# Pairwise products of a batch row: two batch rows at a time, tensor_tensor on VectorE, and less on ScalarE

## The chip, the cores and the metric

The kernel runs on one core of one Trainium2 chip. The metric is device time in microseconds (us) of one execution. A profile, taken in one further execution, records each instruction and each DMA packet. The engines that matter here are VectorE (DVE in the profile), ScalarE (ACT), SyncE (SP, whose queue issues all transfers) and the core's 16 DMA engines.

## The reference

The input is a matrix of 4096 rows (the batch) by 256 columns in float32. For each batch row, every product of two of its elements i and j with j not below i is wanted, in the order of the upper triangle: first the row's element 0 times elements 0 to 255, then element 1 times elements 1 to 255, and so on to element 255 times itself.

```
dot = jnp.einsum('bi,bj->bij', inputs, inputs)     # inputs: (4096, 256) float32
iu, ju = jnp.triu_indices(256)
return dot[:, iu, ju]                              # (4096, 32896) float32
```

The output has 32,896 elements (131,584 bytes) for each batch row, 539 MB in all; the input has 4.2 MB.

## The kernel before

The whole input is held in SBUF, in the tile x. Batch rows lie on the 128 partitions, four neighbouring rows to a partition, so that 512 batch rows make a group and there are eight groups. Three loads on SP's queue (L88) bring the input: group 0, then groups 1 to 3, then groups 4 to 7.

The four output rows of a partition lie one behind the other in HBM, so a group's output is, for each partition, one run of 4 x 32,896 elements. `even_borders` cuts this run into nine pieces of 14,592 or 14,656 elements, regardless of where a row ends. Each piece is made in one buffer of the pool o (three buffers, L79) and written by one transfer from SP's queue (L104): 128 packets of 58,368 or 58,624 bytes, 7,296 or 7,328 KB. Group by group and piece by piece there are 72 pieces. The very first is written in four parts (`FIRST`, L57), so that the first transfer starts early.

`runs` lists the product rows that lie in a piece: product row i of a batch row is x[i] times x[i], x[i+1], up to x[255], so it has 256 - i elements. Each is made by one instruction, in which the factor x[i] is a scalar for each partition. `Shares.multiply` (L44) gives it to VectorE, as a tensor_scalar (L49), or to ScalarE, as an activation with a scale (L52), whichever by its estimate would be done first:

```
v = self.vector + 130 + 0.51 * length
s = self.scalar + 187 + 0.83 * length
```

Both estimates start from zero at each piece (L96). No order is written by hand: each engine takes its instructions in program order, and the tile framework adds the waits. An o buffer can be written again when the transfer that read it has landed; a transfer is issued when both engines have made their part of the piece. SP's queue holds the three loads and then the output transfers in order.

Of the kernel before, what the change touches and what calls it, by code (L numbers as in the profile page):

```python
# [1 line left out]

# [4 lines left out]

F32 = mybir.dt.float32
AF = mybir.ActivationFunctionType
ALU = mybir.AluOpType  # L10

P = 128
UNIT = 64


def even_borders(lo: int, hi: int, pieces: int) -> list[int]:
    units = (hi - lo) // UNIT
    return [lo + units * c // pieces * UNIT for c in range(pieces)] + [hi]


def runs(d: int, lo: int, hi: int):


    width = d * (d + 1) // 2
    for row in range(lo // width, (hi + width - 1) // width):
        at = row * width
        for i in range(d):
            a, b = max(at, lo), min(at + d - i, hi)
            if a < b:
                yield row, i, i + a - at, a, b - a  # L30
            at += d - i


class Shares:


    def __init__(self, nc):
        self.nc = nc
        self.vector = self.scalar = 0.0

    def even(self):
        self.vector = self.scalar = 0.0

    def multiply(self, dst, src, factor, length: int):  # L44
        v = self.vector + 130 + 0.51 * length
        s = self.scalar + 187 + 0.83 * length
        if v <= s:
            self.vector = v
            self.nc.vector.tensor_scalar(dst, src, factor, None, ALU.mult)  # L49
        else:  # L50
            self.scalar = s
            self.nc.scalar.activation(dst, src, AF.Copy, scale=factor)  # L52


REPEAT = 4
PIECES = 9
FIRST = [1024, 3072, 7168]  # L57


@with_exitstack  # L60
def kernel(
    ctx: ExitStack, tc: tile.TileContext, x: bass.AP, out: bass.AP
):

    nc = tc.nc
    n, d = x.shape
    width = out.shape[1]  # L70
    assert n % (P * REPEAT) == 0 and width == d * (d + 1) // 2
    groups = n // (P * REPEAT)
    total = REPEAT * width
    assert total % UNIT == 0
    borders = even_borders(0, total, PIECES)
    slot = max(b - a for a, b in zip(borders, borders[1:]))

    xpool = ctx.enter_context(tc.tile_pool(name="x", bufs=1))
    opool = ctx.enter_context(tc.tile_pool(name="o", bufs=3))  # L79

    x_in = x.rearrange("(g p r) d -> p g r d", p=P, r=REPEAT)
    x_out = out.rearrange("(g p r) c -> g p (r c)", p=P, r=REPEAT)

    xt = xpool.tile([P, groups, REPEAT, d], F32, name="x")
    cuts = sorted({0, 1, groups // 8, groups // 2, groups})
    for a, b in zip(cuts, cuts[1:]):
        if a < b:
            nc.sync.dma_start(xt[:, a:b], x_in[:, a:b])  # L88

    shares = Shares(nc)  # L90
    for g in range(groups):
        for c, (lo, hi) in enumerate(zip(borders, borders[1:])):
            o = opool.tile([P, slot], F32, tag="o", name=f"o_{g}_{c}")
            cuts = [lo, *FIRST, hi] if g == c == 0 else [lo, hi]
            for a, b in zip(cuts, cuts[1:]):
                shares.even()  # L96
                for row, i, j, at, length in runs(d, a, b):
                    shares.multiply(
                        o[:, at - lo : at - lo + length],
                        xt[:, g, row, j : j + length],  # L100
                        xt[:, g, row, i : i + 1],
                        length,
                    )
                nc.sync.dma_start(x_out[g][:, a:b], o[:, a - lo : b - lo])  # L104


# [1 line left out]
_INS = ["r_inputs"]  # L108
_OUTS = [((4096, 32896), "float32")]


# [20 lines left out]
```

## Time and profile before

| | |
|---|---|
| median of 9 runs | 1287.81 us (1287.65 to 1287.94) |
| the profiled execution's own time | 1287.74 us |
| span of its profile | 1286.0 us |
| VectorE busy, instructions | 977.1 us, 4961 |
| ScalarE busy, instructions | 968.3 us, 3299 |
| data moved by DMA, mean rate | 543.71 MB, 423 GB/s |
| issue to landing of a 7,296 KB transfer (median of 39) | 41.9 us |
| issue to landing of a 7,328 KB transfer (median of 32) | 35.9 us |
| first input (512 KB), issue to landing | 3.4 us |

The span runs from the first to the last instruction of the profiled execution; its own time also has what lies before and after. An engine's busy time counts overlapping instructions once, so it can be less than their number times the mean duration of one. "L49 DVE ... o<-x 128x256 f32" reads: line 49 of the kernel, on VectorE, writes tile o from tile x, 128 partitions by 256 elements; "+53 forms" says that the group has other sizes too; behind the bar stand the busy time, the mean duration in ns, and the idle time just before these instructions with what ended it. Of the DMA queues, q1 carries the kernel's own transfers and q14 the engines' instructions. In the table of windows the columns are the stretch, its length, busy time and number of instructions for VectorE, ScalarE and GpSimd, the granted clock of TensorE (not used here), the busy share of the DMA engines and the rate in GB/s.

### The profile page before, as it was taken

To read this page: it belongs to the slowest core of one execution; us is meant where nothing else is said; L and a number is where in the kernel's file an instruction comes from. 1 tells how busy PE (TensorE), PEld (TensorE's weight loads), DVE (VectorE), ACT (ScalarE), POOL (GpSimd) and SP (SyncE) were. 2 spreads that over 40 slices of the span, in tenths; PEclk is the share of its full clock that TensorE was granted. 3 is DMA by queue.
4 is the path that set the end of the run, shared out by engine and by line. 5 is a ranking of instruction groups with operands and counts; after the bars stand their busy time and mean duration, and the time that the engine had idled before them with its cause. 6 is when DMAs were issued, how large, how long until landed. Compare 5 with 4: busy or idle time off the path is not lost.

```text
span 1286.0 us, 8601 instructions
## 1 busy us (share of the span) xinstructions
DVE 977.1 (76%) x4961; ACT 968.3 (75%) x3299; POOL 0.2 (0%) x4
## 2 busy tenths in 40 slices
DVE  8987778777777777777777777777777777688760
ACT  9987778777777777777777777777777777687760
POOL 0000000000000000000000000000000000000000
DMA  9999999999999999999999999999999999999995
GB/s 392 435 435 433 437 431 427 428 431 435 433 435 436 437 435 433 437 426 434 421 435 437 413 433 434 417 430 413 435 410 437 434 411 412 437 435 434 413 408 222
DMA packets 11938, 543.71 MB, mean 423 GB/s; under 512 B 1248, under 2 KB 1248, under 8 KB 2400
## 3 DMA queue, kind: packets, MB, share of 16 engines
q1 hardware_dynamic: 11872, 543.17, 98.0%
q14 instruction: 66, 0.54, 0.1%
HBM read 4.19 MB, written 538.97 MB: 422 GB/s over the span
## 4 chain that ended last, share of the span: by engine, by line
DMA 66%; DVE 31%; issue 0%; DVEq 0%; SPq 0%
DMA out_dram<-o 65%; DVE o L49 31%; DMA x<-in_r_inputs_dram 0%; DVEq L49 0%; SPq L104 0%; DVEq L128 0%
## 5 line engine op out<-in xcount | busy, mean ns | idle before, releaser
L49 DVE TENSOR_SCALAR o<-x 128x256 f32<-128x256 f32 (+53 forms) x4961 | 977.1, 281 | 274.2 <-DMA out_dram<-o 269.9
L52 ACT ACTIVATE o<-x 128x255 f32<-128x255 f32 (+62 forms) x3298 | 967.0, 387 | 282.2 <-DMA out_dram<-o 279.9
L52 ACT ACT_TABLE_LOAD x1 | 1.3, 1283 | 0.7 <-PEq L119 0.7
L119 POOL MEMSET const-bfloat16-1.0<- 128x1 bf16 x1 | 0.1, 102 | 0.0
L119 POOL MEMSET const-uint8-127<- 128x1 uint8 x1 | 0.1, 102 | 0.0
L119 POOL MEMSET const-float32-0.0<- 128x1 f32 x1 | 0.1, 99 | 0.2 <-issue 0.2
L119 POOL MEMSET const-float32-1.0<- 128x1 f32 x1 | 0.1, 99 | 0.0
## 6 DMA issues: line engine op xcount, KB each, us to landing
out_dram<-o SPq DMA_DIRECT2D x39, 7296.0 KB, 41.9
out_dram<-o SPq DMA_DIRECT2D x32, 7328.0 KB, 35.9
out_dram<-o SPq DMA_DIRECT2D x1, 3712.0 KB, 17.8
x<-in_r_inputs_dram SPq DMA_DIRECT2D x1, 2048.0 KB, 12.7
out_dram<-o SPq DMA_DIRECT2D x1, 2048.0 KB, 14.2
x<-in_r_inputs_dram SPq DMA_DIRECT2D x1, 1536.0 KB, 7.2
out_dram<-o SPq DMA_DIRECT2D x1, 1024.0 KB, 12.1
x<-in_r_inputs_dram SPq DMA_DIRECT2D x1, 512.0 KB, 3.4
```

The costliest lines, as they stand in the source:

```text
L49: self.nc.vector.tensor_scalar(dst, src, factor, None, ALU.mult)
L52: self.nc.scalar.activation(dst, src, AF.Copy, scale=factor)
L119: nc = _bacc.Bacc("TRN2", target_bir_lowering=False, num_devices=1)
```

## The change

The layout, the size of the pieces and the way the products are made all change.

- A partition now holds 32 neighbouring batch rows, and a group is two of them (`REPEAT = 2`), so there are 16 groups of 256 batch rows. The input loads are the first group (512 elements for each partition), the rest of the first half, and the second half. The tile x gets one element more, set to zero by a memset.
- A piece is now a stretch of the 32,896 output elements, the same for both batch rows of the group. There are five pieces of 6,528 or 6,592 elements for each batch row; a transfer writes two packets of 26,112 or 26,368 bytes for each partition, and there are 80 pieces. There are still three buffers of o. The first piece is again written in four parts.
- For each block of product rows, `split` gives the first (longest) rows to ScalarE, as few as leave VectorE within `BUDGET` x the number of elements in the block, 1.08 ns for each; in the first piece the two engines are balanced instead.
- `vector_ops` chooses how VectorE makes a product row: "each" is one tensor_scalar for each batch row as before; "all" is one tensor_tensor for both batch rows, whose second operand is x[i] read again and again with a step of zero; "two" is one tensor_tensor that makes product rows i and i+1 of both batch rows. In the last case the pattern has 2 x 2 x (256 - i) elements, although product row i+1 is one shorter: the one element too many is overwritten by the next product row.
- `interleave` cuts the block's rows in two halves and takes VectorE's instructions from them in turn.

The number of bytes moved in and out stays the same, as does the arithmetic of every product.

```diff
--- before.py
+++ after.py
@@ -11,6 +11,10 @@
 
 P = 128
 UNIT = 64
+REPEAT = 2
+PIECES = 5
+BUDGET = 1.08
+FIRST = [512, 1536, 3584]
 
 
 def even_borders(lo: int, hi: int, pieces: int) -> list[int]:
@@ -18,43 +22,75 @@
     return [lo + units * c // pieces * UNIT for c in range(pieces)] + [hi]
 
 
-def runs(d: int, lo: int, hi: int):
+def runs(d: int, lo: int, hi: int) -> list:
 
 
-    width = d * (d + 1) // 2
-    for row in range(lo // width, (hi + width - 1) // width):
-        at = row * width
-        for i in range(d):
-            a, b = max(at, lo), min(at + d - i, hi)
-            if a < b:
-                yield row, i, i + a - at, a, b - a
-            at += d - i
+    found, at = [], 0
+    for i in range(d):
+        a, b = max(at, lo), min(at + d - i, hi)
+        if a < b:
+            found.append((i, i + a - at, a, b - a))
+        at += d - i
+    return found
 
 
-class Shares:
+def vector_ops(block: list) -> list:
 
 
-    def __init__(self, nc):
-        self.nc = nc
-        self.vector = self.scalar = 0.0
-
-    def even(self):
-        self.vector = self.scalar = 0.0
-
-    def multiply(self, dst, src, factor, length: int):
-        v = self.vector + 130 + 0.51 * length
-        s = self.scalar + 187 + 0.83 * length
-        if v <= s:
-            self.vector = v
-            self.nc.vector.tensor_scalar(dst, src, factor, None, ALU.mult)
-        else:
-            self.scalar = s
-            self.nc.scalar.activation(dst, src, AF.Copy, scale=factor)
 
 
-REPEAT = 4
-PIECES = 9
-FIRST = [1024, 3072, 7168]
+
+    ops, k = [], 0
+    while k < len(block):
+        i, j, at, n = block[k]
+        two = k + 2 < len(block) and i == j
+        each = REPEAT * (130 + 0.52 * n)
+        together = 68 + 1.046 * REPEAT * n - (34 if two else 0)
+        if each <= together:
+            ops.append(("each", block[k]))
+        elif two:
+            ops.append(("two", block[k]))
+            k += 1
+        else:
+            ops.append(("all", block[k]))
+        k += 1
+    return ops
+
+
+def interleave(block: list) -> list:
+
+
+    half = len(block)
+    while half and len(vector_ops(block[:half])) > len(vector_ops(block[half:])):
+        half -= 1
+    a, b = vector_ops(block[:half]), vector_ops(block[half:])
+    return [op for k in range(max(len(a), len(b))) for ops in (a, b) for op in ops[k : k + 1]]
+
+
+def vector_time(block: list) -> float:
+    t = 0.0
+    for way, (i, j, at, n) in vector_ops(block):
+        if way == "each":
+            t += REPEAT * (130 + 0.52 * n)
+        else:
+            t += 68 + 1.046 * REPEAT * n * (2 if way == "two" else 1)
+    return t
+
+
+def split(block: list, budget: float) -> int:
+
+
+    scalar, k = 0.0, 0
+    while k < len(block):
+        scalar += REPEAT * (184 + 0.837 * block[k][3])
+        if vector_time(block[k:]) <= budget or scalar > vector_time(block[k + 1 :]):
+            break
+        k += 1
+    return k
+
+
+def window(ap: bass.AP, free: list) -> bass.AP:
+    return bass.AP(ap.tensor, ap.offset, [list(ap.ap[0]), *free])
 
 
 @with_exitstack
@@ -68,40 +104,64 @@
     nc = tc.nc
     n, d = x.shape
     width = out.shape[1]
-    assert n % (P * REPEAT) == 0 and width == d * (d + 1) // 2
+    assert n % (P * REPEAT) == 0 and width == d * (d + 1) // 2 and width % UNIT == 0
     groups = n // (P * REPEAT)
-    total = REPEAT * width
-    assert total % UNIT == 0
-    borders = even_borders(0, total, PIECES)
+    borders = even_borders(0, width, PIECES)
     slot = max(b - a for a, b in zip(borders, borders[1:]))
 
     xpool = ctx.enter_context(tc.tile_pool(name="x", bufs=1))
     opool = ctx.enter_context(tc.tile_pool(name="o", bufs=3))
 
-    x_in = x.rearrange("(g p r) d -> p g r d", p=P, r=REPEAT)
-    x_out = out.rearrange("(g p r) c -> g p (r c)", p=P, r=REPEAT)
+    x_in = x.rearrange("(p r) d -> p (r d)", p=P)
+    x_out = out.rearrange("(p g r) c -> g p r c", p=P, r=REPEAT)
 
-    xt = xpool.tile([P, groups, REPEAT, d], F32, name="x")
-    cuts = sorted({0, 1, groups // 8, groups // 2, groups})
+
+    total = n // P * d
+    xt = xpool.tile([P, total + 1], F32, name="x")
+    nc.vector.memset(xt[:, total:], 0.0)
+    cuts = [0, REPEAT * d, total // 2, total]
     for a, b in zip(cuts, cuts[1:]):
-        if a < b:
-            nc.sync.dma_start(xt[:, a:b], x_in[:, a:b])
+        nc.sync.dma_start(xt[:, a:b], x_in[:, a:b])
 
-    shares = Shares(nc)
     for g in range(groups):
         for c, (lo, hi) in enumerate(zip(borders, borders[1:])):
-            o = opool.tile([P, slot], F32, tag="o", name=f"o_{g}_{c}")
-            cuts = [lo, *FIRST, hi] if g == c == 0 else [lo, hi]
+            o = opool.tile([P, REPEAT, slot], F32, tag="o", name=f"o_{g}_{c}")
+            first = g == c == 0
+            cuts = [lo, *(FIRST if first else []), hi]
             for a, b in zip(cuts, cuts[1:]):
-                shares.even()
-                for row, i, j, at, length in runs(d, a, b):
-                    shares.multiply(
-                        o[:, at - lo : at - lo + length],
-                        xt[:, g, row, j : j + length],
-                        xt[:, g, row, i : i + 1],
-                        length,
+                block = runs(d, a, b)
+                k = split(block, 0.0 if first else BUDGET * REPEAT * (b - a))
+                for i, j, at, length in block[:k]:
+                    for r in range(REPEAT):
+                        row = (g * REPEAT + r) * d
+                        nc.scalar.activation(
+                            o[:, r, at - lo : at - lo + length],
+                            xt[:, row + j : row + j + length],
+                            AF.Copy,
+                            scale=xt[:, row + i : row + i + 1],
+                        )
+                row = g * REPEAT * d
+                for way, (i, j, at, length) in interleave(block[k:]):
+                    at -= lo
+                    if way == "each":
+                        for r in range(REPEAT):
+                            row_r = row + r * d
+                            nc.vector.tensor_scalar(
+                                o[:, r, at : at + length],
+                                xt[:, row_r + j : row_r + j + length],
+                                xt[:, row_r + i : row_r + i + 1],
+                                None,
+                                ALU.mult,
+                            )
+                        continue
+                    m = 2 if way == "two" else 1
+                    nc.vector.tensor_tensor(
+                        o[:, :, at : at + m * length],
+                        window(xt[:, row + j :], [[d, REPEAT], [1, m], [1, length]]),
+                        window(xt[:, row + i :], [[d, REPEAT], [1, m], [0, length]]),
+                        ALU.mult,
                     )
-                nc.sync.dma_start(x_out[g][:, a:b], o[:, a - lo : b - lo])
+                nc.sync.dma_start(x_out[g][:, :, a:b], o[:, :, a - lo : b - lo])
 
 
 # ---- launch: one core; inputs and outputs as the reference has them ----
```

## The prediction

> **What bounds the kernel now.** I read the share of each engine first, then the DMA queues, then the waits, then the trace in windows. From the page of the kernel before:
>
> ```profile
> DVE 977.1 (76%) x4961; ACT 968.3 (75%) x3299; POOL 0.2 (0%) x4
> ...
> q1 hardware_dynamic: 11872, 543.17, 98.0%
> q14 instruction: 66, 0.54, 0.1%
> ...
> L49 DVE TENSOR_SCALAR o<-x 128x256 f32<-128x256 f32 (+53 forms) x4961 | 977.1, 281 | 274.2 <-DMA out_dram<-o 269.9
> L52 ACT ACTIVATE o<-x 128x255 f32<-128x255 f32 (+62 forms) x3298 | 967.0, 387 | 282.2 <-DMA out_dram<-o 279.9
> ```
>
> VectorE and ScalarE idle a quarter of the time, nearly all of it waiting for an output transfer to release one of three o buffers. The 16 DMA engines are 98% busy. So transfers set the time. But a mean hides which engine is last. The windows by stretch (DMA share and GB/s in the last two columns):
>
> ```profile
> 100.00:700.00 600.00, 460.75 (x2338) 456.12 (x1554) 0.00 (x0) 1.00 1.00 433
> 750.00:1250.00 500.00, 382.99 (x1953) 379.19 (x1300) 0.00 (x0) 1.00 0.99 426
> 1271.00:1276.00 5.00, 0.00 (x0) 0.00 (x0) 0.00 (x0) 1.00 0.14 59
> 1277.00:1281.00 4.00, 0.00 (x0) 0.00 (x0) 0.00 (x0) 1.00 0.07 29
> ```
>
> Until 700 us all engines are busy; later the rate drops; after 1271 us two engines work, after 1277 us one (29 GB/s is one sixteenth of the rate). I therefore took from the trace every DMA packet (queue, start, duration, bytes) and the 16 completions of each transfer. How many us the three slowest engines complete after the median one:
>
> | transfer at | slowest (A) | second | third |
> |---|---|---|---|
> | 136 us | 3.6 | 2.0 | 1.2 |
> | 412 us | 10.4 | 6.4 | 4.2 |
> | 688 us | 16.4 | 11.3 | 7.1 |
> | 1252 us | 17.2 | 8.1 | 1.1 |
>
> A loses 2.4 us per 100 us until the others, out of released buffers, must wait for it. The end at 1286 us is A's end. What delays engines is in the packets. A 58,368-byte packet takes 2154 ns. The instruction queue's 8,192-byte packets take 309 ns each, and the data packet right after one takes 440 to 475 ns too long where they follow each other every 33 us (38 times: 4961 VectorE instructions in blocks of 128), and 175 to 200 ns too long where they come every 50 us (24 times: ScalarE). So A carries VectorE's instruction stream at 309+447-4 = 752 ns a block: 22 blocks by 720 us are 16.5 us, against a lag of 17.1. Engine B carries ScalarE's, at 490 ns. A third, C, has no such packets; its data packets are 20 to 60 ns too long, more with more VectorE instructions: mean 29 ns with 8 ending inside a packet, 45 with over 11, and none once both engines have stopped.
>
> [...] queue 14's packets sit between data packets. [...] 433 GB/s is measured from 100 to 700 us[...]. [...] the new distance between partitions is 32 rows of 131,584 bytes, 4 MiB + 16 KiB (before: 512 KiB + 2 KiB).
>
> **The change, part by part.** A's budget before, in us: first packet 3.1; 64 input packets of 159 ns, 9.9; output 1241.1 (8 packets in each of 71 transfers at 2150 or 2160 ns start to start, plus 17.3 for the divided first tile); 78 completions of 5 ns, 0.4; 38 instruction blocks, 28.6. Sum 1283.1; 2.9 us stay unexplained to the span of 1286.0, and I carry them over. The profiled execution took 1287.74, 1.7 outside the span; the median of the runs is 1287.81.
>
> *Smaller packets.* Two rows of 26,112 or 26,368 bytes a partition take the place of one run. From 16,384 bytes in 611 ns and 29,696 in 1100 the slope is 36.73 ns per 1,000 bytes: 968.3 and 977.7 ns, 4 less start to start. Sixteen pairs of rows times 16 packets: 256 x (964.3 + 4 x 973.7) = 1243.9, and 0.1 for the divided first tile: +2.9. Completions and the 6,740 KB transfers hardly count: 86 by 5 ns, 0.4.
>
> *Fewer instructions.* Working the rules of the new planner through: a pair of rows needs 184 VectorE instructions (84 tensor_scalar, 100 tensor_tensor) and 48 on ScalarE; in all 2929 and 786 against 4961 and 3298. 2929/128 is 22.9 blocks; before, 38.8 gave 38, so 22 times 752 ns, 16.5: -12.0. ScalarE's 6 blocks cost B 3 us. C's surplus before is 1276.9-3.1-9.9-1241.1-0.4-2.9 = 19.5 us; by instruction count (3715 of 8259) it becomes 8.8. A stays last: C ends 7.7 us before it. The 752 ns I leave unchanged; if the 447 belonged to the packet's size it would be 200 ns (16.5 falls to 11), and without it A has 7 us and C (8.8) ends last.
>
> *VectorE's work.* Per pair of rows its planned time is 70.3 us (13.8 to 14.2 per tile). tensor_scalar's 130 + 0.52n fits the trace: 4961 x 130 ns plus 0.51 for some 640,000 elements gives 971, measured 977. tensor_tensor is not in the trace. [...] A needs (1244.4+16.5)/16 = 78.8 us per pair. I take the plan, because the trace's tensor_scalars overlap: 281 ns each but 197 busy. All of it then lies beneath the transfers: a tile's product starts when the transfer three back lands and needs 14.2 us, while two transfers of 15.6 stand queued. Without the cover each us over 78.8 counts 16 times. A tensor_tensor of two rows writes one element too many, which the next one overwrites, so each may wait on its forerunner in its half; behind it stands only VectorE's own queue, then SP's output issue. The halves alternate, so another instruction of mostly over 200 ns lies between; [...] I take nothing.
>
> *ScalarE's work* falls to 13.7 us in each pair's 79[...]. *Input:* 2 KB, 14 KB and 16 KB packets, 9.7 against 9.9; first products start about 0.6 us sooner, hidden by input transfers to 12.8 us. *Start:* the first tile's pieces keep their 512 KB, 1, 2 and the rest; VectorE ends it at about 3.6+9.6 = 13.2, the second tile at 27.5[...], while the first tile's transfers end at 28.4: some 0.5 us lost (0 to 2). The memset of one column precedes the first landing.
>
> Sum for A: 3.1+9.7+1244.0+0.4+16.5+2.9+0.5 = 1277.1-1277.3, plus 1.7: **1279.0 us**, 0.7% faster. Its own range is 1271 (C last, no penalty packets) to 1283.
>
> **The rivals.**
> *VectorE becomes the bound.* At 85 ns over the plan per tensor_tensor the pair takes VectorE 78.8 us. A VectorE-bound end has the first input (3.6), the last transfer with its landing (17.5) and 1.7 around it: at that point 1284, then 1.6 us for each further ns. From 89 ns (over 1290.4) it is slower[...]. For it: 100 unseen instructions per pair, each perhaps waiting. Against it: the alternation and the overlap seen. I say 1300 where it happens, chance 0.09.
> *C's surplus doesn't follow the instruction count.* If it is per time VectorE is busy (76% to 88%), 19.5 becomes 22.6: 3.1+9.7+1244+0.4+22.6+2.9+0.5+1.7 = 1285. If per packet, the half-size packets (26 ns each in the trace) say 1280 x 26 = 33 us: 1295.6. Against it: surplus rises with endings at a full VectorE (29 to 45 ns), and is gone in the tail. Chance 0.07.
> *The instruction stream doesn't shrink as counted.* Were each tensor_tensor to bring a wait instruction (1600 more, 35 blocks), A gains 9.8: 1288.8. Before, only some 260 of 8601 are beyond the named groups. Chance 0.04.
> *Row distance.* [...] at a tenth less rate, about 1405. [...] Chance 0.04.
>
> **How the numbers follow.** The forecast has 0.76. Under 0.2% is about what this kernel's measurement can't tell from no change (1285.2 to 1290.4). Faster: 0.75 of the forecast, 0.04 of C's rival: 0.79. Same: 0.01 + 0.01 + 0.03 of the stream's + 0.03 of VectorE's: 0.08. Slower, the rest: 0.13. The range 1271 to 1288 takes in the forecast's own (0.75), C by time, the first of VectorE's and part of the stream's rival: 0.82.
>
> **What would show it.** Queue 14 with some 30 packets, VectorE 2929 instructions and busy near 1120 us, ScalarE 786 and near 226; output packets of 968 and 978 ns; A's lag growing 1.3 us per 100 us and a tail of one engine at about 27 GB/s, some 8 us long. Wrong would be: VectorE without idle on output transfers and DMA share below 0.95 midway (first rival); C last (second); queue 14 above 45 packets (third); DMA full at under 420 GB/s midway (fourth).

## The result, and the profile after

The changed kernel takes 1277.98 us (median of 9 runs, 1277.74 to 1278.24) against 1287.74 us before (29 runs): a ratio of 0.9924, 95% interval 0.9916 to 0.9932. It is 0.76% faster. The prediction was 1279.0 us. The profiled execution took 1277.78 us with a span of 1276.0 us.

From the page of the changed kernel (busy time by engine, the DMA queues, and the groups of instructions):

```profile
DVE 1129.0 (88%) x2978; ACT 234.7 (18%) x787; POOL 0.2 (0%) x4
...
q1 hardware_dynamic: 23008, 543.17, 99.6%
q14 instruction: 32, 0.26, 0.0%
...
L158 DVE TENSOR_TENSOR o<-x 128x104 f32<-128x104 f32 (+60 forms) x1651 | 804.7, 560 | 59.2 <-DMA out_dram<-o 59.2
L137 ACT ACTIVATE o<-x 128x197 f32<-128x197 f32 (+25 forms) x786 | 233.5, 384 | 1000.5 <-DMA out_dram<-o 904.2
L149 DVE TENSOR_SCALAR o<-x 128x216 f32<-128x216 f32 (+5 forms) x1326 | 345.3, 335 | 53.0 <-DMA out_dram<-o 50.0
```

VectorE now works 88% of the time, longer than before, and still waits 109 us for released buffers: the transfers set the time, as before. What fell is the traffic of queue 14, from 66 packets to 32.

The windows of the changed kernel (the last two columns are the DMA share and GB/s):

```profile
100.00:700.00 600.00, 544.76 (x1434) 110.06 (x374) 0.00 (x0) 1.00 1.00 430
750.00:1250.00 500.00, 442.92 (x1182) 93.27 (x318) 0.00 (x0) 1.00 1.00 430
1265.00:1270.00 5.00, 0.00 (x0) 0.00 (x0) 0.00 (x0) 1.00 0.47 200
1271.00:1275.00 4.00, 0.00 (x0) 0.00 (x0) 0.00 (x0) 1.00 0.05 20
```

Two things stand against the windows of before. The rate no longer drops halfway (430 and 430, where it was 433 and 426), because the slowest engine no longer falls so far behind that the others wait for it (7.3 us behind the median engine at the last transfer, where it was 15.0). And the end is still one engine alone, but for some 5 us, where it was some 9. The rate of 430 in the first stretch is lower than the 433 of before; that is the one thing in these lines which the prediction did not have.

The packets of the trace, at the three slowest engines' completions, say the same: A is 1.9 us behind the median engine at 170 us, 4.5 us at 719 us, 7.3 us at the last transfer; the second and third end 2.5 and 1.1 us behind. The trace doesn't name the DMA engine of a packet, but on one engine each packet starts where the one before ends (3 to 4 ns before its recorded end). Followed back in this way from its end, the last engine has the instruction packet of 1233.1 us on it, and behind that a data packet 386 ns too long: VectorE's stream.

### The profile page after: what moved, and what is told of

It is laid out like the page before. It is cut to its first block, busy times and chain, and to the rows that moved or that the text cites. A ratio compares the mean times of both kernels' runs of the same rounds, so it can differ in the third digit from the quotient of the medians.

```text
span 1276.0 us, 4106 instructions
## 1 busy us (share of the span) xinstructions
DVE 1129.0 (88%) x2978; ACT 234.7 (18%) x787; POOL 0.2 (0%) x4
## 4 chain that ended last, share of the span: by engine, by line
DMA 60%; DVE 37%; issue 0%; DVEq 0%; SPq 0%
DMA out_dram<-o 59%; DVE o L158 26%; DVE o L149 11%; DMA x<-in_r_inputs_dram 0%; SPq L164 0%; DVEq L158 0%; DVEq L149 0%; DVEq L188 0%
## 5 line engine op out<-in xcount | busy, mean ns | idle before, releaser
L158 DVE TENSOR_TENSOR o<-x 128x104 f32<-128x104 f32 (+60 forms) x1651 | 804.7, 560 | 59.2 <-DMA out_dram<-o 59.2
L137 ACT ACTIVATE o<-x 128x197 f32<-128x197 f32 (+25 forms) x786 | 233.5, 384 | 1000.5 <-DMA out_dram<-o 904.2
L149 DVE TENSOR_SCALAR o<-x 128x216 f32<-128x216 f32 (+5 forms) x1326 | 345.3, 335 | 53.0 <-DMA out_dram<-o 50.0
```

What stands on the lines that cost most here:

```text
L137: nc.scalar.activation(o[:, r, at - lo : at - lo + length], xt[:, row + j : row + j + length], AF.Copy, scale=xt[:, row + i : row + i + 1],)
L149: nc.vector.tensor_scalar(o[:, r, at : at + length], xt[:, row_r + j : row_r + j + length], xt[:, row_r + i : row_r + i + 1], None, ALU.mult,)
L158: nc.vector.tensor_tensor(o[:, :, at : at + m * length], window(xt[:, row + j :], [[d, REPEAT], [1, m], [1, length]]), window(xt[:, row + ...
```

## The experiments

The theory: the time is that of the DMA engine A which, beside its sixteenth of the data, brings VectorE's instructions. Each block of 128 instructions (38 blocks for 4961 in the kernel before) costs it a packet of 309 ns and a delay of the next data packet (that packet takes longer than others of its size, by 447 ns on average in the kernel before). The change gained by its smaller number of VectorE instructions. The rivals: the layout brought the gain (fewer rows per partition, two packets, another distance of the rows in HBM); the work of VectorE and ScalarE or the number of all instructions matters, not the stream of one engine.

All times are medians of the comparison with the kernel before on the same chip.

| run | us | ratio to before (95% interval) |
|---|---|---|
| changed kernel | 1277.98 | 0.9924 (0.9916 to 0.9932) |
| e1, new layout, old number of instructions | 1290.32 | 1.0020 (1.0012 to 1.0028) |
| e2, other row distance | 1278.82 | 0.9930 (0.9917 to 0.9942) |
| e3, more on VectorE, placed ahead | 1408.89 | 1.0940 (1.0925 to 1.0955) |
| e4, more on ScalarE, placed ahead | 1320.53 | 1.0254 (1.0240 to 1.0268) |
| e5, halves not alternating | 1321.06 | 1.0259 (1.0244 to 1.0274) |
| e6, transfers alone, old layout | 1260.70 | 0.9790 (0.9776 to 0.9805) |
| e7, transfers alone, new layout | 1269.96 | 0.9862 (0.9847 to 0.9877) |
| e8, budget 0.75 | 1274.85 | 0.9900 (0.9883 to 0.9916) |
| e9, no tensor_scalar, budget 0.9 | 1273.26 | 0.9888 (0.9874 to 0.9901) |
| e10, e8 with 1520 more on VectorE | 1282.64 | 0.9961 (0.9948 to 0.9973) |
| e11, e8 with 1520 more on ScalarE | 1278.03 | 0.9925 (0.9911 to 0.9938) |
| e12, old layout, fewer instructions | 1275.96 | 0.9908 (0.9892 to 0.9925) |

### The two halves of the change apart: e1 and e12

e1 keeps the new layout and makes each product by its own instruction, shared evenly between the engines:

```diff
-                block = runs(d, a, b)
-                k = split(block, 0.0 if first else BUDGET * REPEAT * (b - a))
-                ...
+                v = s = 0.0
+                for r in range(REPEAT):
+                    row = (g * REPEAT + r) * d
+                    for i, j, at, length in runs(d, a, b):
+                        ...
+                        if v + 130 + 0.51 * length <= s + 187 + 0.83 * length:
+                            v += 130 + 0.51 * length
+                            nc.vector.tensor_scalar(dst, src, factor, None, ALU.mult)
+                        else:
+                            s += 187 + 0.83 * length
+                            nc.scalar.activation(dst, src, AF.Copy, scale=factor)
```

> The new layout (two rows, five pieces, packets of 26 KB) with one instruction for each product row and batch row, both engines balanced as in the kernel before; so about 4990 VectorE and 3300 ScalarE instructions. Theory (the DMA engine that carries VectorE's instruction stream ends last): 39 blocks in place of 24, at 309 ns and some 366 ns of delay each, 671 ns: 26.2 us in place of 16.1, so 1288 us, and a tail of one engine. Rival (the layout, its packets or the row distance brought the gain): about 1278 us.

It took 1290.32 us. From its page, and its windows at the end:

```profile
DVE 984.5 (76%) x5013; ACT 969.1 (75%) x3315; POOL 0.2 (0%) x4
...
q14 instruction: 68, 0.56, 0.1%
```

```profile
1280.00:1285.00 5.00, 0.00 (x0) 0.00 (x0) 0.00 (x0) 1.00 0.06 26
```

The instruction packets are back (68), and so is an engine that works alone (26 GB/s) until 1287 us. Its last 105 packets contain two instruction packets, and data packets that are 376 to 443 ns too long. The 39 delays of VectorE's stream average 402 ns here, not 366: 39 x (309 + 402 - 4) = 27.6 us, so A's sum is 3.1 + 9.7 + 1244.0 + 0.4 + 27.6 + 2.9 + 1.8 = 1289.5 us. The layout by itself makes the kernel 2.6 us slower (1290.32 against 1287.75); the rival falls.

e12 is the other half: the layout and the packets of before, with tensor_tensors of two product rows of one batch row on VectorE, in alternating halves, and the longest rows of a piece on ScalarE:

```diff
-                shares.even()
-                for row, i, j, at, length in runs(d, a, b):
-                    shares.multiply(...)
+                block = list(runs(d, a, b))
+                scalar = share(block, SCALAR * (b - a) / slot)     # SCALAR = 13500.0, longest rows first
+                ...
+                for m, (row, i, j, at, length) in interleave(rest):
+                    ...
+                        nc.vector.tensor_tensor(
+                            dst,
+                            window(xf[:, base + j :], [[1, 2], [1, length]]),
+                            window(xf[:, base + i :], [[1, 2], [0, length]]),
+                            ALU.mult,
+                        )
```

> The kernel before, its layout and its packets of 58 KB kept, with fewer instructions: VectorE makes two neighbouring product rows of one batch row by one tensor_tensor (halves alternating as in the changed kernel), ScalarE takes the longest rows of each piece up to 13.5 us. 2912 instructions on VectorE and 2728 on ScalarE by count. Theory: 22 blocks at 752 ns, 16.5 us: 3.1 + 9.9 + 1241.1 + 0.4 + 16.5 + 2.9 + 1.7 = 1275.6 us, less than the changed kernel's 1278. Rival (the two-row layout is needed for the gain): 1288 us.

It took 1275.96 us. From its page:

```profile
DVE 756.0 (59%) x2920; ACT 967.3 (76%) x2728; POOL 0.2 (0%) x4
...
q14 instruction: 46, 0.38, 0.1%
```

So fewer instructions alone, in the old layout, save 11.7 us; the whole change saves 9.8. ScalarE is as busy as in the kernel before (967 us), so it isn't relief of ScalarE that counts. VectorE's busy time fell too, from 977 to 756 us; that this is not what counts is shown by the order of the runs below ("Fewer still"). One part of the expectation did not hold: by the packets, A ends at 1272.2 us (eight instruction packets from 824 us on, with delays of 404 to 462 ns behind them, can be followed on it), and the last, 0.75 us later, is an engine without instruction packets whose data packets are 26 ns too long on average. It fits what the prediction called C; see below.

### One instruction more, on one engine or the other: e3, e4, e10 and e11

e3 and e4 add 19 instructions of one element to each piece, written to a tile of their own:

```diff
+                for _ in range(19 if b == hi else 0):
+                    nc.vector.tensor_scalar(tiny[:, count % 64 : count % 64 + 1], xt[:, 0:1], xt[:, 1:2], None, ALU.mult)
+                    count += 1
```

> The changed kernel with 19 more tensor_scalars of one element in each of the 80 pieces, 1520 in all, which write a tile that nothing reads. Theory: 1520/128 is 11.9 blocks more in the stream of VectorE, 671 ns each: 8.0 us, 1286 us, though VectorE still waits for released buffers in most pieces. Rival (VectorE's instructions cost nothing while it has idle time): 1278 us.

> The same with 1520 more activations of one element on ScalarE. Theory: they go to the other DMA engine, at 309 and some 113 ns a block: 6 + 12 blocks are 7.5 us there, less than the 16.1 us of the engine with VectorE's stream, so no change: 1278 us. Rival (every instruction delays the transfers alike, whatever its engine): 1283 to 1286 us.

They took 1408.89 and 1320.53 us and answer another question than the one asked. The windows of e3, first for the added instructions alone (their busy time and number on VectorE, then clock, DMA share and GB/s) and then for all:

```profile
50.00:400.00 350.00, 99.00 (x804) 1.00 0.81 346
400.00:700.00 300.00, 79.34 (x645) 1.00 0.80 344
700.00:1000.00 300.00, 0.00 (x0) 1.00 1.00 429
```

```profile
50.00:400.00 350.00, 350.00 (x1494) 52.80 (x181) 0.00 (x0) 1.00 0.81 346
400.00:700.00 300.00, 300.00 (x1237) 42.88 (x146) 0.00 (x0) 1.00 0.80 344
700.00:1000.00 300.00, 275.85 (x734) 54.67 (x186) 0.00 (x0) 1.00 1.00 429
```

The added instructions wait for nothing, so the framework moved all of them ahead, to before 634 us; until then VectorE has no idle time (350.00 us busy of 350.00, 300.00 of 300.00), its work is longer than the transfers, and the DMA share is 0.8. In e4 they fill ScalarE until some 350 us in the same way (from 200 to 300 us they take 86.73 us of it, with a DMA share of 0.78). Both runs show what it costs when an engine becomes the bound, and nothing about streams.

e10 and e11 repeat the test on e8 (below), which leaves both engines room, and write the elements into spare columns of the piece's own buffer, so that they can't be moved ahead:

```diff
-            o = opool.tile([P, REPEAT, slot], F32, tag="o", name=f"o_{g}_{c}")
+            o = opool.tile([P, REPEAT, slot + 32], F32, tag="o", name=f"o_{g}_{c}")
+                for q in range(19 if b == hi else 0):
+                    dst = o[:, 1, slot + q : slot + q + 1]
+                    nc.vector.tensor_scalar(dst, xt[:, 0:1], xt[:, 1:2], None, ALU.mult)     # e11: nc.scalar.activation
```

> The balanced kernel (budget 0.75, 1274.85 us) with 19 more tensor_scalars of one element in each of the 80 pieces, 1520 in all, written into spare columns of the piece's own buffer, so that they can't be moved ahead of it; these columns are not transferred. They take VectorE 2.3 us per piece, of some 5 that it waits there. Theory: 11.9 blocks more in VectorE's stream at 671 ns, 8.0 us: 1282.8 us. Rival (VectorE's instructions cost nothing while it has idle time): 1275 us.

> The balanced kernel with the same 1520 instructions put on ScalarE instead, as activations of one element. Theory: ScalarE's stream has 29 blocks at 309 + 113 ns, 12.2 us, about the 11.7 us of VectorE's on its engine, and the third slow engine gains 3.5 us: 1275 to 1278 us. Rival (every instruction delays the transfers alike, whatever its engine): 1282.8 us.

From the pages of e10 and of e11:

```profile
DVE 1021.8 (80%) x3730; ACT 718.9 (56%) x2211; POOL 0.2 (0%) x4
...
L145 DVE TENSOR_SCALAR o<-x 128x1 f32<-128x1 f32 x1520 | 191.4, 205 | 222.5 <-DMA out_dram<-o 222.4
```

```profile
DVE 838.1 (66%) x2210; ACT 1002.0 (79%) x3731; POOL 0.2 (0%) x4
...
L145 ACT ACTIVATE o<-x 128x1 f32<-128x1 f32 x1520 | 291.1, 282 | 0.0
```

On VectorE the 1520 instructions cost 7.8 us (1282.64 against 1274.85), 0.65 us for each of 12 blocks (queue 14 has 49 packets in place of 37), though VectorE idles on output transfers for 222 us in front of them. The expected 8.0 us is met, and the last engine carries an instruction packet with a delay of 363 ns behind it. On ScalarE they cost 3.2 us (1278.03), at the edge of what was expected, and less than half of VectorE's price; so the engine whose instructions they are matters. Part of the difference in price is room: in e8 the three slowest DMA engines complete the last transfer 5.6, 5.1 and 3.7 us behind the median, so one that isn't last can take on some time before it sets the end. Which DMA engine ends last in e11 I could not follow for more than 20 packets: ScalarE's stream or C may be it.

### What protects VectorE: e5

e5 makes the product rows of a piece in order, without the two halves in turn:

```diff
-                for way, (i, j, at, length) in interleave(block[k:]):
+                for way, (i, j, at, length) in vector_ops(block[k:]):
```

> The changed kernel without the alternation of the two halves: VectorE makes the product rows of a piece in order, so each tensor_tensor overwrites the last element of the one right before it. If each then waits for its forerunner, [...] 1284 to 1289 us, and VectorE hardly waits for buffers. If the alternation does nothing: 1278 us and the same 1129 us busy.

It took 1321.06 us, beyond the range given. From its page:

```profile
DVE 1248.5 (95%) x2930; ACT 234.7 (18%) x787; POOL 0.2 (0%) x4
...
L158 DVE TENSOR_TENSOR o<-x 128x248 f32<-128x248 f32 (+49 forms) x1603 | 917.1, 580 | 48.6
```

The 1603 tensor_tensors last 580 ns each, 929.7 us in sum, and are busy for 917.1: they hardly overlap. With the halves alternating, 1651 of 560 ns (924.6 in sum) are busy for 804.7. Besides, 48.6 us of gaps stand in front of them, with no transfer as releaser. The trace shows the wait: in both kernels most tensor_tensors wait for a semaphore that VectorE's own instructions raise (1440 of 1651 in the changed kernel, 1488 of 1603 in e5). In e5 a tensor_tensor behind another starts 34 ns after its end (median of 1568); in the changed kernel, where the one it overwrites lies further back, 82 ns before it (1520). Two tensor_tensors in succession can overlap as such: in e9 (below), which has no other products on VectorE and lets the halves alternate, it is 83 ns. So a tensor_tensor that overwrites the last element of the one before it waits for it. VectorE's time for a pair of rows becomes (1248.5 + 48.6)/16 = 81.1 us against 78.8 of transfers, and the prediction's first rival, with its own formula, gives 3.6 + 16 x 81.1 + 17.5 + 1.7 = 1320.4 us. The loss is some 105 ns for each tensor_tensor ((1248.5 + 48.6 - 1129.0) us over 1603), more than the range of e5 allowed for; that range was the author's estimate. The order of the instructions is what keeps that rival away.

### The transfers alone: e6 and e7

Two tensor_scalars fill each piece; the products are left out. The edit of e7 (e6 does the same in the old layout, one tensor_scalar for each half of a piece):

```diff
-                ...
+                for r in range(REPEAT):
+                    nc.vector.tensor_scalar(
+                        o[:, r, a - lo : b - lo], xt[:, : b - a], xt[:, row : row + 1], None, ALU.mult
+                    )
```

> The layout and the packets of the kernel before, without its products: two large tensor_scalars fill each piece with multiples of input elements, ScalarE does nothing. What is left is the transfers with almost no instruction stream. Theory: 3.1 + 9.9 + 1241.1 + 0.4 + 2.9 + 1.7 = 1259 us, up to 1264 us if engines that run together lengthen each other's packets by 7 ns as after 750 us in the kernel before. Rival (something else than the streams holds the kernel before back): above 1270 us.

> The same for the layout and packets of the changed kernel: no products, two large tensor_scalars in each piece. Theory: 3.1 + 9.7 + 1244.0 + 0.4 + 2.9 + 1.7 = 1262 us if packets take 964 and 974 ns from start to start, 1270 us if the 6 to 7 ns that the engines running together show in the changed kernel stay (1280 packets an engine). Rival (VectorE's work or its stream lengthens them): 1262 us.

They took 1260.70 and 1269.96 us. From the pages of e6 and of e7:

```profile
DVE 574.1 (46%) x150; POOL 0.2 (0%) x4
...
q1 hardware_dynamic: 11872, 543.17, 99.9%
q14 instruction: 3, 0.02, 0.0%
```

```profile
DVE 576.9 (45%) x167; POOL 0.2 (0%) x4
...
q1 hardware_dynamic: 23008, 543.17, 100.1%
q14 instruction: 3, 0.02, 0.0%
```

With almost no instruction packets, the old layout is 27.0 us faster than the kernel before, about what A's surplus was put at (28.6 us). And the new layout's transfers take 9.3 us longer than the old one's, not 2.9: in e7 the packets of 26,112 and 26,368 bytes take 968 and 978 ns until some 200 us, and from then on 7 ns more on average. The rival of e7 that VectorE's instruction stream lengthens them falls, as there is hardly any. Its work is still there (45% of the time), but finds no support as the cause: in the changed kernel, with 88%, the packets are lengthened by no more (6.4 ns on average from 300 us on, without the delayed ones, against 6.9).

### Row distance: e2

e2 puts neighbouring pairs of batch rows on neighbouring partitions, so that the partitions lie 257 KiB apart in the output; the input loads are written to match:

```diff
-    x_in = x.rearrange("(p r) d -> p (r d)", p=P)
-    x_out = out.rearrange("(p g r) c -> g p r c", p=P, r=REPEAT)
+    x_in = x.rearrange("(g p r) d -> p g (r d)", p=P, r=REPEAT)
+    x_out = out.rearrange("(g p r) c -> g p r c", p=P, r=REPEAT)
...
```

> The changed kernel with neighbouring row pairs on neighbouring partitions, so that partitions lie 2 rows (257 KiB) apart in the output and no longer 32 rows (4.1 MiB); the input comes in packets of 2 KB. Theory: 1278 to 1279 us (at most 0.6 us more for the input packets). Rival (the row distance plays a part, gain or loss): off by more than 0.2%, or output packets that differ from 968 and 978 ns and from the means of 975 and 985 ns.

It took 1278.82 us, 0.8 us above the changed kernel, and its packets have the same shortest times and, after some 300 us, the same means to within 1 ns. Against 257 KiB, the changed kernel's distance of 4 MiB + 16 KiB costs nothing that shows.

### Fewer still: e8 and e9

e8 sets `BUDGET` to 0.75; e9 sets it to 0.9 and replaces the test of `vector_ops` by one that never chooses tensor_scalar:

```diff
-        if each <= together:
+        if False:
```

> The changed kernel with a budget of 0.75 ns per element in place of 1.08: more of the long rows go to ScalarE, some 2200 instructions remain on VectorE and some 2200 on ScalarE. Theory: 17 blocks in place of 24 at 671 ns, 4.7 us less: 1273.3 us; ScalarE's 17 blocks at 418 ns stay below. Rival (the number of instructions in all counts, 4400 against 3765): slower than 1278 us.

> The changed kernel with no tensor_scalar at all (every product row of VectorE goes by tensor_tensor) and a budget of 0.9 ns per element: some 1730 instructions on VectorE and 1760 on ScalarE. Theory: 13 blocks at 671 ns, 8.7 us, about what the longer packets cost the other engines (the transfers alone take 1270 us with this layout), so no engine ends last by much: 1270 to 1272 us. Rival (VectorE's busy time or something else sets the end): 1274 us or more.

From the pages of e8 and of e9:

```profile
DVE 837.6 (66%) x2210; ACT 718.9 (56%) x2211; POOL 0.2 (0%) x4
```

```profile
DVE 946.6 (74%) x1766; ACT 564.4 (44%) x1767; POOL 0.2 (0%) x4
```

1274.85 us: e8 has more instructions in all than the changed kernel (4420 against 3764) and is 3.1 us faster; the rival of the total falls. It missed its 1273.3 by 1.6 us; what those are is not shown. e9 took 1273.26 us and is the fastest of the complete kernels, 1.1% below the kernel before and 4.7 us below the changed one, but 1.3 us above its range. With VectorE's stream cut to 14 blocks of 661 ns (9.3 us), A's sum is 1271.1 us; two us are not explained, and which engine ends last could not be settled from the packets.

Apart from e11, with its additions on ScalarE, the complete kernels of the new layout that the transfers bound stand in the order of VectorE's instructions (e9 1766, e8 2210, changed kernel and e2 2978, e10 3730, e1 5013: 1273.26, 1274.85, 1277.98 and 1278.82, 1282.64, 1290.32 us). They don't stand in the order of its busy time (947, 838, 1129, 1022, 985 us). That answers the rival of VectorE's work.

## Why the prediction was right

**What bounds the kernel.** Right. A, the engine with VectorE's stream, sets the end in the kernel before, the changed kernel, e1 and e10, and the price of a block is measured from outside by e10 (0.65 us). In its sum one term has a wrong name: the first packet of the kernel before starts 1.7 us into the span and the last ends at 1284.6, so that of the "first packet 3.1" some 1.3 us lie behind the last packet; the packet times of the prediction and of its table are later than the span's by as much. The sum and the forecast don't change.

**Fewer instructions.** Right in the sum, 24 x (309 + 369 - 4) ns = 16.2 us against the 16.5 predicted, by two errors that cancel: that the sum came so close is luck. There are 2978 VectorE instructions and not 2929, since the alternation plans each half by itself (1651 tensor_tensors, not 1603), and 24 blocks were fetched, not 22. And the delay behind a block fell from 447 to 369 ns, which the prediction had left unchanged with a smaller value as its lower end. The mean delays of VectorE's blocks by run:

| | denser instructions | fewer |
|---|---|---|
| packets of 58 KB | 447 ns (before) | 417 ns (e12) |
| packets of 26 KB | 402 ns (e1) | 369 ns (changed kernel) |

So the delay is smaller with smaller packets and with fewer instructions; why is not shown.

**Smaller packets.** For A the step holds: its packets behind the instruction packets take 968 and 978 ns, as worked out. For the other engines it is too small. Their packets are 6 to 7 ns longer, which over 1280 packets is 8 us. Hence A's lag grew by 0.6 us per 100 us and not by 1.3, and the 7.3 us by which A ends behind the median are all that a shorter stream could still bring (4.8 us until ScalarE's engine is reached; e9 gained 4.7). The time itself is A's, so this didn't move the forecast.

**C's surplus by instruction count.** It did not decide: the second engine at the end, 2.5 us behind the median, carries ScalarE's stream (its last instruction packet, at 1232.4 us, is followed to its end), and the third-slowest completion of the last transfer is 1.1 us behind. But e12 measures C's surplus, if the engine that ends last there is C: 1274.4 - 3.1 - 9.9 - 1241.1 - 0.4 - 2.9 = 17.0 us with 5648 instructions, where 19.5 x 5648/8259 = 13.3 was to be expected. So it does not simply follow the count; its law, and what C carries, stay open.

**VectorE's work.** The plan's price for tensor_tensor, the author's estimate, held in the sum: 1129 us busy against some 1120. A single tensor_tensor lasts longer than that price (1043 ns for 856 elements in the trace, where 68 + 1.046 x 856 gives 963), but with the halves alternating they overlap: 924.6 us in sum are busy for 804.7. That this hangs on the alternation, as the prediction argued, is shown by e5. The first rival was nearer than its chance of 0.09 says: without the alternation it comes true, at the 1320.4 us of its formula and not at the 1300 that the prediction put on it.

**The other rivals.** The stream shrank (32 packets of queue 14, "some 30" were predicted); the row distance is without effect that shows (e2, 1278.82 us against 1277.98). The start's 0.5 us was the author's estimate and was not tested apart; with the measured stream, A's sum without it is 1276.3 us against a span of 1276.0, so it does not show.

## What to carry to other kernels

When the DMA engines are full, look at which of them ends last and what else it carries: here the instructions of VectorE, fetched in blocks of 128, cost 0.65 us (e10) to 0.75 us (kernel before) per block on the one DMA engine that brings them, though VectorE had idle time (222 us in front of e10's added instructions). So in a transfer-bound kernel, cut the number of instructions, first on the engine with the most expensive stream (1520 more cost 7.8 us on VectorE and 3.2 us on ScalarE), and pay for that with busy time that lies beneath the transfers (VectorE went from 977 to 1129 us). Order instructions that overwrite a piece of their forerunner's output so that another one stands between; without that, e5 lost some 105 ns on each and took 1321.06 us in place of 1277.98.

## What had not been expected

In these runs the packets of engines that run in step become longer in the course of an execution. In e6 (58 KB) they take 2154 and 2164 ns without exception until some 200 us, with few exceptions until 600 us, and from 700 us on 5 to 6 ns more on average; in e7 (26 KB) the change comes at some 220 us, in the changed kernel between 50 and 110 us, in e12 (58 KB) before 100 us. It stays until the end, is of about the same size for both lengths of packet (5 to 7 ns), so counts twice for packets half as long, and hardly shows on an engine that lags far behind the others (A in the changed kernel). What sets it off is not known. With it the new layout's transfers alone take 9.3 us more than the old one's, so that the two parts of this change work against each other: in the old layout fewer instructions give 1275.96 us (e12), and 1260.7 us would be left if there were none.
